# A graph layer on one core: 63 columns a chunk by the engines instead of 119, and no single rows by SP

## The chip, the cores and the metric

The kernel runs on one core of one Trainium2 chip. The core has a matrix engine (PE, TensorE), a vector engine (DVE), an activation engine (ACT), a general engine (POOL, GpSimd) and a queue engine (SP) that issues transfers and computes nothing. Each engine works through its own instructions in order; engines wait for one another through semaphores. The engines' sequencers can hold numbers in registers, and an instruction or a transfer can take its address from a register.

The metric is the time of one execution in microseconds (us), on the device. Lower is better. All times below come from the runs and the profiled execution of this kernel.

## The reference

There are 12,500 nodes with 48 features, 400,000 edges sorted by their destination, and 32 features per edge. In short:

```python
h = maximum(layernorm(x), 0)                       # 12500 x 48
tmp = concatenate([h[dst], h[src], edge_attr], 1)  # 400000 x 128
hid = relu(tmp @ W1 + b1)                          # 400000 x 128
msg = hid @ W2 + b2                                # 400000 x 48
out = x + segment_sum(msg, dst, 12500)             # 12500 x 48
```

`dst` is sorted, so that the edges of one stretch go to few nodes; `src` is random, so that each edge needs a row of its own.

## The kernel before

The product with `W1` is split by its three inputs. Two tables are made once, at the start: `tab_a` holds, for every node, `h @ W1[:48] + b1`, and `tab_b` holds `h @ W1[48:96]`. Both lie in DRAM (HBM), a row of 128 numbers (512 bytes) per node. The same numbers as `tab_b` are also kept in SBUF, turned, as `bt`: a column of 128 numbers per node.

The edges are then worked through in 391 chunks of 8 tiles, a tile being 128 edges (3125 tiles in all; the last chunk has 5). The main loop (L487 to L527) has one round per chunk `c` and two more, and it is written out in full; the order of each engine's instructions is the order in which the Python code calls them. One round touches three chunks:

- `prepare(c)` (L355) issues the loads of chunk `c`. SP loads one number (which node the chunk's window begins at), then issues the transfers for `rhs` (80 rows of `tab_a` from that node on), for the edge features into `lhs` and for the destinations (`row`). POOL issues one gather per tile: an indirect transfer of 128 rows of `tab_b`, by the tile's `src`, into `gb` (L376). DVE then makes two one-hot matrices, `lhs` (L383) and `hot` (L388).
- `before(c-1)` (L395) lets PE multiply `lhs` with `rhs` into `pre` (16 matmuls at L401): the parts of the sum that come from `dst` and from the edge features.
- `hidden(c-1)` (L415) adds the gathered rows: DVE writes `hid = pre + gb` (L420), and ACT applies the relu (L425).
- `fold(c-2)` (L428) lets PE sum the chunk's `hid` by destination within a window of 80 nodes (L433, L438), and `add(c-2)` (L443) lets DVE add that to a longer segment in SBUF (L452). Every 12 chunks a segment is multiplied with `W2`, added to `x` and stored (L456 to L484).

`gb` has six buffers (`gp`, L713). A gather for chunk `c` writes the buffer that chunk `c-6` had, so POOL can run ahead of the other engines until it has to wait for DVE's `hid` of that earlier chunk.

Not all tiles are gathered by POOL. There are two other ways:

- **Columns.** For one tile in most chunks DVE and ACT fetch the 128 columns from `bt`, one instruction per edge: `columns` (L341) copies one column of `bt`, whose address is in a register, into a column of a tile `gt` (L353). PE then adds `gt` to `pre`, turned back by a matmul with the identity (`turned`, L407; L411), and ACT applies the relu to that tile straight from `pre` (L424). The numbers of the edges' source nodes stand in a table `last` in SBUF, a row per chunk, and `load` (L329) brings them into registers with one instruction per up to 32 numbers (`numbers`, L300; the instruction has line L304). `PARTS` (L55) shares 119 columns a chunk: DVE does three parts of 23, 20 and 16, ACT two of 28 and 32. The loop places each part by hand: part 0 between `lhs` and `hot`, parts 1 and 2 ahead of `hidden`, part 3 (ACT) just ahead of `hidden`, part 4 (ACT) behind it. The register loads stand a part or more ahead of the copies.
- **Rows.** For 45 further tiles SP fetches the 128 rows from `tab_b` one at a time: `rows` (L314) issues 15 transfers of 512 bytes a chunk (L322) into a tile `gs`, each address from a register, and DVE adds `gs` in `hidden` by an instruction of its own (L422).

## Time and profile before

| | |
|---|---|
| median of 3 runs | 5028.71 us (5015.86 to 5036.02) |
| profiled execution | 5046.97 us, its span 5045.2 us |
| busy share of the span: PE, DVE, ACT, POOL | 63%, 58%, 58%, 53% |
| mean granted TensorE clock | 0.643 |
| gathers by POOL (L376) | 2719 |
| one-column copies (L353): DVE, ACT | 22,928 and 23,280 |
| single rows by SP (L322) | 5760 |

In the rows of the profile a line number stands for the line of the kernel; `out<-in` names what an instruction writes and reads; `128x896 f32` is partitions by elements. A group has its count (`x2719`), then the busy time in us and the mean of one in ns, and behind the second bar the time that its engine stood idle just before its instructions, with what ended it. "issue" is written where the profile shows nothing that the engine waited for. In the order of time each row has a start and a length in us (several like instructions in a row are merged, with their count), and in brackets the idle time before it. A q behind an engine's name (DVEq) marks what the engine's sequencer does itself, such as loading registers. In a row for a stretch of time (`A:B length, ...`) five pairs follow, the busy us and the count of instructions of PE, of PE's weight loads, of DVE, of ACT and of POOL, and then the granted clock, the share of the transfer engines and GB/s. Stretches, starts and lengths are counted from the start of the span.

### The profile page before, as it was taken

The numbers are of one execution on the slowest core, as the hardware profiler recorded it, in microseconds if no ns is written. First come the engines' busy times: TensorE is split into PE (matmuls) and PEld (weight loads), VectorE is DVE, ScalarE is ACT, GpSimd is POOL, SyncE is SP. The second block draws the span as 40 slices with busy tenths as digits, with TensorE's granted clock in tenths as the row PEclk, the third lists the DMA queues.
The fourth block names the chain that finished last, engine by engine and source line by source line (L and its number), as shares of the span: only waits on it lengthen the run. The fifth ranks groups of instructions, "written<-read, shape, count | busy, mean of one in ns | idle before, by whom it ended". The sixth has DMA issues, their size and how long they took to land. (4 is left out here: it accounts for less than half of the span.)

```text
span 5045.2 us, 105760 instructions
## 1 busy us (share of the span) xinstructions
PE 3196.2 (63%) x16917; PEld 2891.6 (57%) x16917; DVE 2915.2 (58%) x24786; ACT 2927.7 (58%) x24107; POOL 2664.5 (53%) x2746
## 2 busy tenths in 40 slices
PE   6565666665666665566666665666666666666676
PEld 4555555555555555556565555556555565555565
DVE  4555555555555555565555555555555565555555
ACT  3455655655555555566565555556565566555555
POOL 5455555555555555555555555555555555555553
PEclk8666666666666666666666666666666666665656
DMA  3422222222222222222222222222222222222221
GB/s 135 123 67 69 68 66 68 68 67 68 64 65 66 68 70 67 64 68 71 67 69 69 68 67 67 69 67 69 67 67 68 69 71 68 68 66 69 66 69 51
DMA packets 202255, 354.44 MB, mean 70 GB/s; under 512 B 70322, under 2 KB 108228, under 8 KB 200276
## 3 DMA queue, kind: packets, MB, share of 16 engines
q0 software_dynamic: 87040, 178.39, 14.2%
q1 hardware_dynamic: 114256, 169.09, 11.3%
q14 instruction: 560, 4.59, 0.3%
q8 instruction: 139, 2.28, 0.2%
q10 hardware_dynamic: 260, 0.10, 0.0%
HBM read 327.84 MB, written 22.07 MB: 69 GB/s over the span
## 5 line engine op out<-in xcount | busy, mean ns | idle before, releaser
L376 POOL DMA_INDIRECT gb<-tab_b,srci x2719 | 2643.0, 972 | 2315.4 <-DVE hid L420 1319.5
L353 ACT COPY gt<-bt 128x1 f32 x23280 | 2477.9, 189 | 1893.8 <-issue 1867.1
L353 DVE COPY gt<-bt 128x1 f32 x22928 | 1704.1, 143 | 1795.4 <-issue 1750.0
L433 PE MATMUL p_g<-hot,hid 128*128 128x80 f32 x6250 | 1392.9, 414 | 1664.1 <-ACT hid L425 1585.3
L433 PEld LDWEIGHTS p_g<-hot,hid 128*128 128x128 f32 x6250 | 1313.3, 320 | 1745.7 <-ACT hid L425 1689.4
L401 PEld LDWEIGHTS pre<-rhs,lhs 112*128 112x128 f32 x6250 | 1149.6, 283 | 92.8 <-issue 85.4
L401 PE MATMUL pre<-rhs,lhs 112*128 112x128 f32 x6250 | 1171.3, 366 | 17.1 <-DVE lhs L383 17.1
L420 DVE TENSOR_TENSOR hid<-pre,gb 128x896 f32<-128x896 f32 (+2 forms) x391 | 420.8, 1076 | 6.8 <-issue 4.4
L425 ACT ACTIVATE hid<-hid 128x896 f32<-128x896 f32 (+1 forms) x391 | 370.8, 948 | 39.3 <-DVE hid L420 38.0
L411 PE MATMUL pre<-ident,gt 128*128 128x128 f32 x722 | 278.7, 489 | 112.0 <-remote 104.9
L388 DVE TENSOR_TENSOR hot<-wnum,rel 128x640 f32<-128x640 f32 x391 | 315.9, 808 | 5.1 <-issue 4.9
L383 DVE TENSOR_SCALAR lhs<-row,bw 80x1024 f32<-80x1024 int16 x391 | 306.8, 785 | 12.8 <-DMA row<-in_dst 7.9
L438 PEld LDWEIGHTS <-ones 128*128 128x128 bf16 x3125 | 291.9, 154 | 0.0
L438 PE MATMUL p_g<-hot,ones 128*128 128x80 bf16 x3125 | 283.7, 265 | 0.0
L411 PEld LDWEIGHTS pre<-ident,gt 128*128 128x128 f32 x722 | 193.4, 328 | 118.4 <-remote 110.6
L452 DVE TENSOR_TENSOR seg<-seg,p_g 128x160 f32 x391 | 125.7, 321 | 191.8 <-DVE hid L420 156.8
L424 ACT ACTIVATE hid<-pre 128x128 f32<-128x128 f32 x361 | 97.5, 270 | 86.8 <-DVE hid L420 78.4
L478 PE MATMUL p_f<-seg,w2s 128*48 128x512 f32 (+1 forms) x134 | 121.0, 1005 | 0.4 <-DVE seg L452 0.4
L479 PE MATMUL p_f<-seg,b2s 1*48 1x512 f32 (+1 forms) x134 | 95.5, 801 | 0.0
L479 PEld LDWEIGHTS p_f<-seg,b2s 1*48 1x48 f32 x134 | 13.1, 143 | 100.8 <-issue 100.8
L468 DVE MEMSET seg<- 128x944 f32 x64 | 54.1, 845 | 9.5 <-issue 0.3
L480 DVE TENSOR_TENSOR xseg<-xseg,p_f 48x512 f32<-48x512 f32 (+1 forms) x67 | 44.8, 668 | 23.3 <-PE p_f L479 22.4
(67 smaller groups left out, 306.3 us busy)
## 6 DMA issues: line engine op xcount, KB each, us to landing
gs<-tab_b SPq DMA_DIRECT2D x5760, 0.5 KB
row<-in_dst SPq DMA_DIRECT2D x390, 160.0 KB
lhs<-in_edge_t SPq DMA_DIRECT2D x390, 128.0 KB
gb<-tab_b,srci POOLq DMA_INDIRECT x2719
rhs<-tab_a SPq DMA_DIRECT2D x391, 40.0 KB
xseg<-in_x_t SPq DMA_DIRECT2D x33, 192.0 KB
out_x<-xseg SPq DMA_DIRECT2D x33, 192.0 KB
tab_b<-tab SPq DMA_DIRECT2D x3, 1280.0 KB
```

The costliest lines, as they stand in the source:

```text
L353: copy(gts[of][:, e : e + 1], bt8[:, bass.ds(at, 4)].bitcast(F32))
L376: nc.gpsimd.indirect_dma_start(out=gb[:, t, :], out_offset=None, in_=tab_b[:, :], in_offset=bass.IndirectOffsetOnAxis(ap=srci[:, c * T + t ...
L383: nc.vector.tensor_scalar(lhs[:W, : n * P], row[:, : n * P], bw[:, c : c + 1], None, op0=ALU.is_equal,)
L388: nc.vector.tensor_tensor(hot[:, :n, :], wnum.unsqueeze(1).to_broadcast([P, n, W]), rel[:, c * T : c * T + n].unsqueeze(2).to_broadcast([P ...
L401: nc.tensor.matmul(pre[:, t, :], s["lhs"][:K, t * P : (t + 1) * P], s["rhs"][:K, :], start=True, stop=c not in BYCOLS or t < n - 1,)
L411: nc.tensor.matmul(s["pre"][:, s["n"] - 1, :], gts.pop(c), ident, start=False, stop=True)
L420: nc.vector.tensor_add(h[:, :g, :], pre[:, :g, :], s["gb"][:, :g, :])
L425: nc.scalar.activation(h[:, :m, :], h[:, :m, :], AF.Relu)
L433: nc.tensor.matmul(p_g[:, 0, :], s["h"][:, t, :], s["hot"][:, t, :], start=t == 0, stop=t == n - 1)
L438: nc.tensor.matmul(p_g[:, 1, :], ones, high[:, t, 1::2], start=t == 0, stop=t == n - 1)
L452: nc.vector.tensor_add(to, to, s["p_g"])
L478: nc.tensor.matmul(p_f[:, :n], w2s, seg[:, 0, s], start=True, stop=False)
```

## The change

The single rows by SP are gone, with `ROWS0`, `RPART`, `BYROWS`, `rows`, `gs` and the sum at L422; POOL gathers those tiles. The columns become 63 a chunk instead of 119: two parts for DVE (15 and 16) and two for ACT (16 and 16). Each part fits one load of 16 registers (part 0 has the window's base as its sixteenth number). The number table becomes 69 wide instead of 140. `gt` tiles have five buffers instead of three.

The code for the columns becomes more general: a chunk may have no, one or two tiles by columns (`TURNED`, `turned_at`), and the loop runs over as many parts as there are. The loads move: part 0 is loaded just ahead of its copies instead of at the end of the round before. The loop's general lines load and copy the last DVE part (`DVE_PARTS - 1`, here part 1) behind `hidden` and at the end of the round; `load(c, 1)` in `prepare`, behind `hot`, and `columns(c, 1)` behind `prepare` stand as they were.

```diff
 PARTS = (
-    (True, 0, 23, 1), (True, 23, 20, 24), (True, 43, 16, 44),
-    (False, 59, 28, 60), (False, 87, 32, 88),
+    (True, 0, 15, 1),
+    (True, 15, 16, 16),
+    (False, 31, 16, 32),
+    (False, 47, 16, 48),
 )
...
-BASE = 120
-RPART = 15
+BASE = 64
+DVE_PARTS = sum(dve for dve, *_ in PARTS)
+BEHIND = len(PARTS) - 1
...
-WIDTH = 140
+WIDTH = 69
...
-BYROWS = tiles_of(ROWS0, RPART)
+TURNED = {c: [j for j, of in enumerate(BYCOLS) if of == c] for c in set(BYCOLS)}
+
+def turned_at(c):
+    return ((), (T - 1,), (T // 2 - 1, T - 1))[len(TURNED.get(c, ()))]
+
+def gathered_at(c):
+    return [t for t in range(min(T, NT - c * T)) if t not in turned_at(c)]
...
-        gtp = es.enter_context(tc.tile_pool(name="gtp", bufs=3))
+        gtp = es.enter_context(tc.tile_pool(name="gtp", bufs=5))
...
-            m = max(0, min(RPART, len(BYROWS) * P - (c - ROWS0) * RPART)) if c >= ROWS0 else 0
-            base, *nodes = numbers(c, BASE, 1 + m, mybir.EngineType.SP)
+            base, = numbers(c, BASE, 1, mybir.EngineType.SP)
...
-            for t in range(n - (c in BYCOLS) - (c in BYROWS)):
+            for t in gathered_at(c):
                 nc.gpsimd.indirect_dma_start(
...
+            load(c, 0)
             columns(c, 0)
...
             for c in range(NCH + 2):
                 if c < NCH:
                     prepare(c)
-                    rows(c, st[c].pop("rows"))
                 if c >= NCH:
+                    load(c, 0)
                     columns(c, 0)
+                    load(c, 1)
                 columns(c, 1)
-                load(c, 2)
-                columns(c, 2)
+                for part in range(2, DVE_PARTS - 1):
+                    load(c, part)
+                    columns(c, part)
...
-                columns(c, 3)
+                columns(c, DVE_PARTS)
+                for part in range(DVE_PARTS + 1, BEHIND):
+                    load(c, part)
+                    columns(c, part)
                 if 0 <= c - 1 < NCH:
                     hidden(c - 1)
-                load(c + 1, 0)
-                load(c, 4)
-                columns(c, 4)
+                load(c, DVE_PARTS - 1)
+                for part in range(BEHIND, len(PARTS)):
+                    load(c, part)
+                    columns(c, part)
+                load(c + 1, DVE_PARTS)
                 if 0 <= c - 2 < NCH:
                     add(c - 2)
                     if k == GQ - 1:
                         segment_next(g)
-                load(c + 1, 3)
+                columns(c, DVE_PARTS - 1)
```

In `hidden`, a chunk with no or one tile by columns has the same two or three instructions as before: one sum by DVE over the gathered tiles, one relu by ACT over them, and, where there is a tile by columns, one relu straight from `pre`.

More of the change, by code (lines that the diff above doesn't have):

```diff
@@ L50 @@
 COLS = 1
-ROWS0 = 1
 END = NT // T
 PARTS = (
-    (True, 0, 23, 1), (True, 23, 20, 24), (True, 43, 16, 44),
-    (False, 59, 28, 60), (False, 87, 32, 88),
+    (True, 0, 15, 1),
+    (True, 15, 16, 16),
+    (False, 31, 16, 32),
+    (False, 47, 16, 48),
 )
 PART = sum(n for _, _, n, _ in PARTS)
-BASE = 120
-RPART = 15
+BASE = 64
+DVE_PARTS = sum(dve for dve, *_ in PARTS)
+BEHIND = len(PARTS) - 1
 BT0 = 16512
-SEG0 = 122144
+SEG0 = 121024
 SEG_SIZE = 8 * L
-SEG, NEXT, SEG2 = 136, 137, 138
-PLACE0 = 139
-WIDTH = 140
+SEG, NEXT, SEG2 = 65, 66, 67
+PLACE0 = 68
+WIDTH = 69
 SLOTS = (NCH + 2 + P - 1) // P
@@ L263, in windows @@
             )
-        rows_at = slice(BASE, BASE + 1 + RPART)
+        rows_at = slice(BASE, BASE + 1)
         nc.vector.tensor_scalar(
@@ L267, in windows @@
         )
-        tab8, taba8 = (t.rearrange("n h -> (n h)").bitcast(U8) for t in (tab_b, tab_a))
+        taba8 = tab_a.rearrange("n h -> (n h)").bitcast(U8)
         place = PARTS[0][3] - 1
@@ L290, in windows @@
         gts = {}
-        gss = {}
         def group(c):
@@ L312, in node @@
             return n.with_bounds(min_val=0, max_val=N - 1)
-        def rows(c, nodes):
-            for k, n in enumerate(nodes):
-                e = (c - ROWS0) * RPART + k
-                of = BYROWS[e // P]
-                if of not in gss:
-                    gss[of] = gtp.tile([P, HID], F32, name="gs")
-                n = n.with_bounds(min_val=0, max_val=4 * HID * (N - 1))
-                nc.sync.dma_start(
-                    gss[of].bitcast(U8)[e % P : e % P + 1, :],
-                    tab8[bass.ds(n, 4 * HID)].rearrange("(o h) -> o h", o=1),
-                )
         regs = {}
@@ L345, in columns @@
             for k, at in enumerate(regs.pop((c, part), [])):
-                j, e = divmod((c - COLS) * PART + first + k, P)
-                of = BYCOLS[j]
+                of, e = divmod((c - COLS) * PART + first + k, P)
                 if of not in gts:
@@ L372, in prepare @@
             )
-            st[c] = dict(n=n, rows=nodes)
+            st[c] = dict(n=n)
             gb = gp.tile([P, T, HID], F32, name="gb")
-            for t in range(n - (c in BYCOLS) - (c in BYROWS)):
+            for t in gathered_at(c):
                 nc.gpsimd.indirect_dma_start(
@@ L402, in before, with added @@
                     pre[:, t, :], s["lhs"][:K, t * P : (t + 1) * P], s["rhs"][:K, :],
-                    start=True, stop=c not in BYCOLS or t < n - 1,
+                    start=True, stop=t not in turned_at(c),
                 )
-            s["pre"], s["added"] = pre, n - (c in BYCOLS)
+            s["pre"] = pre
         def turned(c):
-            if c in BYCOLS:
-                s = st[c]
-                nc.tensor.matmul(
-                    s["pre"][:, s["n"] - 1, :], gts.pop(c), ident, start=False, stop=True
-                )
+            for t, j in zip(turned_at(c), TURNED.get(c, ())):
+                nc.tensor.matmul(st[c]["pre"][:, t, :], gts.pop(j), ident, start=False, stop=True)
         def hidden(c):
             s = st[c]
-            n, m, pre = s["n"], s["added"], s["pre"]
+            n, pre = s["n"], s["pre"]
             h = wp.tile([P, T, HID], F32, name="hid")
-            g = m - (c in BYROWS)
-            nc.vector.tensor_add(h[:, :g, :], pre[:, :g, :], s["gb"][:, :g, :])
-            if g < m:
-                nc.vector.tensor_add(h[:, g, :], pre[:, g, :], gss.pop(c))
-            if m < n:
-                nc.scalar.activation(h[:, m, :], pre[:, m, :], AF.Relu)
-            nc.scalar.activation(h[:, :m, :], h[:, :m, :], AF.Relu)
+            two = len(turned_at(c)) == 2
+            half = T // 2
+            def added(x, to):
+                if not two:
+                    return x[:, :to, :]
+                return x.rearrange("p (b t) h -> p b t h", b=2)[:, :, : half - 1, :]
+            to = n - len(turned_at(c))
+            nc.vector.tensor_add(added(h, to), added(pre, to), added(s["gb"], to))
+            if two:
+                nc.scalar.activation(
+                    h[:, half - 1 :: half, :], pre[:, half - 1 :: half, :], AF.Relu
+                )
+            elif to < n:
+                nc.scalar.activation(h[:, to, :], pre[:, to, :], AF.Relu)
+            nc.scalar.activation(added(h, to), added(h, to), AF.Relu)
             s["h"] = h
@@ L823 @@
     numbers[:NCH, NEXT] = nxt
-    cols = by_tile[np.array(BYCOLS) * T + T - 1].reshape(-1)
+    cols = by_tile[[c * T + turned_at(c)[TURNED[c].index(j)] for j, c in enumerate(BYCOLS)]].reshape(-1)
     cols = np.pad(cols, (0, -len(cols) % PART)).reshape(-1, PART)
@@ L827 @@
         numbers[COLS : COLS + len(cols), at : at + n] = cols[:, k : k + n]
-    in_rows = np.array(BYROWS) * T + T - 1 - np.isin(BYROWS, BYCOLS)
-    rows = by_tile[in_rows].reshape(-1)
-    rows = np.pad(rows, (0, -len(rows) % RPART)).reshape(-1, RPART)
-    numbers[ROWS0 : ROWS0 + len(rows), BASE + 1 : BASE + 1 + RPART] = rows
     last = np.ascontiguousarray(numbers.reshape(SLOTS, P, WIDTH).transpose(1, 0, 2))
```

## The prediction

> **What bounds the kernel now.** I read the page's engine and group rows first, then POOL's groups over the main loop, then the order of time in one chunk.

> ```profile
> span 5045.2 us, 105760 instructions
> PE 3196.2 (63%) x16917; PEld 2891.6 (57%) x16917; DVE 2915.2 (58%) x24786; ACT 2927.7 (58%) x24107; POOL 2664.5 (53%) x2746
> ...
> L353 ACT COPY gt<-bt 128x1 f32 x23280 | 2477.9, 189 | 1893.8 <-issue 1867.1
> L353 DVE COPY gt<-bt 128x1 f32 x22928 | 1704.1, 143 | 1795.4 <-issue 1750.0
> ...
> gs<-tab_b SPq DMA_DIRECT2D x5760, 0.5 KB
> ```

> No engine is full. DVE and ACT lose some 1.8 ms each in front of one-column copies, and "issue" means that the profile shows nothing they waited for. The next rows are POOL's: its only group between 160 and 4983 us, and the first gathers of the first and of the last chunk that it serves there.

> ```profile
> L376 POOL DMA_INDIRECT gb<-tab_b,srci x2671 | 2597.3, 972 | 2280.8 <-DVE hid L420 1319.5 <-issue 696.5 <-DVE hid L422 165.9
> 160.00 1.02 POOL L376 DMA_INDIRECT gb<-tab_b,srci  x1 [54.35 <-DVE hid L420]
> 4982.88 0.94 POOL L376 DMA_INDIRECT gb<-tab_b,srci  x1 [3.25 <-DVE hid L422]
> ```

> From 160.00 to 4982.88 lie 384 chunks: 4822.9 / 384 = 12.56 us each. POOL's share of one is 2597.3 / 384 = 6.76 us of gathers, 696.5 / 384 = 1.81 us of pauses of 0.30 us between them, and the rest of its idle time, (2280.8 - 696.5 - 54.35) / 384 = 3.98 us, in which it waits until DVE's sum `hid` frees a gather buffer. 6.76 + 1.81 + 3.98 = 12.55: a chunk is **a burst of gathers plus a wait for DVE**. A gather with its pause is (2597.3 + 696.5) / 2671 = 1.233 us. What DVE does meanwhile stands in the order of time of one chunk (start, length, engine, line):

> ```profile
> 3004.75 0.95 POOL L376 DMA_INDIRECT gb<-tab_b,srci  x1 [5.19 <-DVE hid L420]
> 3012.32 0.95 POOL L376 DMA_INDIRECT gb<-tab_b,srci  x1 [0.30 <-issue]
> 3017.59 0.94 POOL L376 DMA_INDIRECT gb<-tab_b,srci  x1 [4.32 <-DVE hid L420]
> 3008.39 0.81 DVE L353 COPY gt<-bt 128x1 f32 x8
> 3009.72 0.15 DVE L353 COPY gt<-bt 128x1 f32 x1 [0.52 <-issue]
> 3014.76 0.34 DVE L353 COPY gt<-bt 128x1 f32 x4 [0.55 <-issue]
> 3015.26 1.06 DVE L353 COPY gt<-bt 128x1 f32 x16 [0.16 <-issue]
> 3016.24 1.08 DVE L420 TENSOR_TENSOR hid<-pre,gb 128x896 f32<-128x896 f32 x1
> 3009.71 0.19 ACT L353 COPY gt<-bt 128x1 f32 x1 [0.45 <-issue]
> 3014.76 2.52 ACT L353 COPY gt<-bt 128x1 f32 x26 [0.51 <-issue]
> ```

> Some 4.2 us after the burst's start (3004.75 to about 3009) DVE and ACT fall into a **slow spell**: single copies, on both engines at the same instants. It ends at 3014.76 on both, 1.49 us after the last gather's end (3012.32 + 0.95). Then DVE has 20 copies left (4 and 16), 1.48 us up to `hid`; `hid` takes 1.08, and POOL starts 0.27 us after it: 1.49 + 1.48 + 1.08 + 0.27 = 4.32, the wait in the third row. Is the spell made by gathers, or by SP's single rows? Three stretches (length; then per engine busy us and count; POOL's is the fifth): a spell with rows, a spell of chunk 385 or later, when the rows are all loaded, and two chunks after the last gather.

> ```profile
> 3008.98:3014.75 5.77, 1.59 (x13) 1.40 (x13) 1.26 (x10) 1.63 (x10) 3.37 (x4) 0.50 0.23 59
> 4975.03:4980.98 5.95, 1.59 (x10) 1.40 (x8) 1.16 (x14) 2.08 (x15) 3.69 (x4) 0.50 0.21 58
> 4993.95:5009.40 15.45, 11.53 (x84) 11.15 (x84) 12.94 (x126) 12.69 (x119) 0.00 (x0) 0.79 0.08 21
> 4970.91 1.22 POOL L376 DMA_INDIRECT gb<-tab_b,srci  x1 [3.83 <-DVE hid L420]
> ```

> Without gathers there is no spell, and a chunk takes 15.45 / 2 = 7.7 us. Without rows the spell stays: 14 and 15 instructions of DVE and ACT in 5.95 us instead of 10 and 10 in 5.77, and the chunk from 4970.91 to 4982.88 takes 11.97 us. So it belongs to the gathers.

> **The change, part by part.** *More gathers.* 361 tiles by columns and 45 by rows become 191 by columns: 389 chunks of 63 columns are 24,507, in tiles of 128. POOL gathers 3125 - 191 = 2934 tiles instead of 2719. Of these 2888 fall to the 385 chunks served from 160 us on (the first six chunks come before): 7.50 a chunk instead of 6.95, 9.25 us instead of 8.57. Nothing hides this, as bursts of 6, 8 and then 7 show:

> ```profile
> 4909.84 1.47 POOL L376 DMA_INDIRECT gb<-tab_b,srci  x1 [4.79 <-DVE seg L452]
> 4920.35 0.95 POOL L376 DMA_INDIRECT gb<-tab_b,srci  x1 [2.79 <-DVE hid L420]
> 4933.97 0.95 POOL L376 DMA_INDIRECT gb<-tab_b,srci  x1 [3.84 <-DVE hid L420]
> ```

> The 6 take 10.51 us from start to start, the 8 take 13.62: the spell only ends after the last gather, so DVE cannot use a longer burst.

> *Fewer copies, but not so few.* The new loop loads and copies part 1 twice: its load stays behind `hot`, the copy stands in front of `hid`, and with two DVE parts the general lines load and copy it again behind `hid`. DVE does 15 + 16 + 16 = 47 copies a chunk, not 31, with three loads of 16 numbers; ACT does 32, with two. DVE's program without a spell is this:

> ```profile
> 4992.26 1.22 DVE L420 TENSOR_TENSOR hid<-pre,gb 128x1024 f32<-128x1024 f32 x1
> ...
> 5000.29 1.08 DVE L420 TENSOR_TENSOR hid<-pre,gb 128x896 f32<-128x896 f32 x1
> 5001.89 0.32 DVE L452 TENSOR_TENSOR seg<-seg,p_g 128x160 f32 x1 [0.52 <-DVE hid L420]
> ...
> 5002.79 1.47 DVE L353 COPY gt<-bt 128x1 f32 x23
> ...
> 5005.09 1.30 DVE L353 COPY gt<-bt 128x1 f32 x20
> 5006.90 1.07 DVE L353 COPY gt<-bt 128x1 f32 x16 [0.51 <-issue]
> 5007.87 1.09 DVE L420 TENSOR_TENSOR hid<-pre,gb 128x896 f32<-128x896 f32 x1
> ```

> From `hid` to `hid` it is 7.58 us. A copy is 0.060 us (1.47 us for 23, each lasting 0.14 and overlapping the next), so 12 fewer save 0.72. The gaps of 0.52 and 0.51 are loads of registers:

> ```profile
> L304 DVEq TENSOR_LOAD <-last x1202: 305/1382/5174, 147.5 to 5032.2; - x172
> L304 ACTq TENSOR_LOAD <-last x776: 1695/1932/2829, 134.8 to 5009.0; - x194
> ```

> (Minimum, median, maximum in ns.) ACT's loads have 28 and 32 numbers, so a number costs (1932 - 1695) / 4 = 59 ns; DVE's have 24, 20 and 16, the median being that of 20. Sixteen take 1382 - 4 × 59 = 1.15 us. Behind `hid` 8 fewer numbers close the gap of 0.52 (0.47 saved); in the other places a load stays beside `lhs`, `hot` or copies, and I save nothing. The program is 7.58 - 0.72 - 0.47 = 6.39 us, of which 6.39 - 1.35 = 5.0 lies behind the burst's start (`hid` starts 1.35 before it). [...]

> So at the spell's start (4.2) DVE has 5.0 - 4.2 = 0.8 us left, about 13 copies, where the spell lets 10 (with rows) to 14 (without) through. Bounds for the 1.48 us that now follow the spell: they go whole, or stay whole if a spell starting earlier passes less. I take zero, the nearer end by this count. ACT finishes its 32 copies likewise, and PE no longer waits for late columns.

> *SP's rows* (14.7 per chunk, behind `rhs`, `lhs` and `row` of the same chunk on SP) go. Nothing waits on SP; the chunk without rows bounds the gain at 12.56 - 11.97 = 0.6 us and the loss at nothing. It has a spell and a leftover of its own, which I have already struck out, so I add nothing. With the rows goes L422, 45 sums in all. *A wider sum*: `hid` has 1024 columns in half the chunks, 1.22 us instead of 1.08: 1.15 on average. *Set-up*, the half-sized number table and two more `gt` buffers: off the loop, zero.

> **Sum.** Wait 1.49 + 0 + 1.15 + 0.27 = 2.91; chunk 9.25 + 2.91 = 12.16 instead of 12.55; 384 × 12.16 = 4669, with 160 us before and 62.3 behind the loop 4892, with 1.8 outside the span 4893. The profiled execution took 5046.97 against a median of 5028.71 (0.4% more), about what one run differs from the next: I forecast 4890.

> **Rivals.** *A: bursts join and the spell deepens (slower).* If `hid` slips out inside the spell, the next burst starts before the spell is over, and DVE's next program meets it from its first copy. Before the loop 44 gathers ran without a break:

> ```profile
> 78.11 2.04 PE L181 MATMUL p_n<-wa,ht 97*128 97x256 f32 x4 [2.22 <-DVE bt L211]
> 87.65 0.59 ACT L190 COPY tab<-p_n 128x512 f32<-128x512 f32 x1 [13.89 <-remote]
> 104.70 0.95 POOL L376 DMA_INDIRECT gb<-tab_b,srci  x1 [0.30 <-issue]
> 109.41 0.59 ACT L190 COPY tab<-p_n 128x512 f32<-128x512 f32 x1 [21.17 <-remote]
> ```

> ACT started 7.5 us after PE's matmuls that it waits for ended (78.11 + 2.04), and the last lag outlived the gathers (104.70 + 0.95) by 3.8 us. If a second burst passes almost nothing, two chunks cost 18.5 + 3.8 + 5.3 (the program without `hid`) + 1.42 = 29.0, 14.5 each, 5790 us; if it passes copies at the usual 10 per 5.77 us, about half the program is done and the pair costs some 24.2, as forecast. Between them, 13.2 a chunk: 5290. It decides once `hid` ends within 1.49 us of the burst's last gather. Against it: no such join in the loop now.

> *B: the wait stays 3.98 (slower).* DVE's and ACT's copies run denser ahead of the spell, it starts earlier, 20 copies stay behind it: 9.25 + 3.98 = 13.23, 5300 us. Break-even is a wait of 12.55 - 9.25 = 3.30.

> *C: no spell (much faster).* The program ends at 5.0; were the spell 1 us later, POOL alone would bound: 384 × 9.3 + 222 = 3790. The rowless chunk speaks against it.

> **Chances.** Forecast with its neighbours (11.4 to 12.45 a chunk, 4600 to 5005) 0.48; A 0.26, B 0.12, C 0.07, no change 0.07. Under 0.5% a measurement of this kernel tells nothing from no change. Range 4590 to 5320; faster 0.55, same 0.07, slower 0.38. The likeliest case's own range is 4600 to 5005.

> **What would show it.** Per chunk: 7.5 gathers; a wait of POOL near 2.9 us; DVE with 0 to 3 copies between spell and `hid`; 47 DVE copies; L304 on DVE near 1.15 us; no gap over 0.15 behind `hid`. I am wrong if bursts of 15 appear (A), if ten or more copies follow the spell (B), or if spells are gone (C).

## The result, and the profile after

The changed kernel takes 5329.71 us (median of four runs, 5326.27 to 5334.81) where the kernel before, beside it, takes 5032.36 (5015.86 to 5038.81): a ratio of 1.0597, with a 95% interval of 1.0569 to 1.0625. It is 6% slower; the forecast was 4890.

In the changed kernel the loop's lines are: gathers L374, copies L352, register loads L317, `lhs` L381, `hot` L387, `hid` L425, the sum into the segment (`seg`) L459. The page of the profiled execution (5331.86 us), engines first, then groups (busy us, mean ns | idle time before them and what ended it):

```profile
span 5330.1 us, 78242 instructions
PE 3224.0 (60%) x16577; PEld 2897.8 (54%) x16577; DVE 2487.8 (47%) x20052; ACT 1731.3 (32%) x13073; POOL 2961.6 (56%) x2961
...
L374 POOL DMA_INDIRECT gb<-tab_b,srci x2934 | 2940.1, 1002 | 2289.7 <-DVE hid L425 1298.0
...
L352 DVE COPY gt<-bt 128x1 f32 x18240 | 1275.0, 144 | 1721.0 <-issue 1673.6
...
L459 DVE TENSOR_TENSOR seg<-seg,p_g 128x160 f32 x391 | 125.5, 321 | 777.5 <-issue 665.7
```

A quarter of the instructions is gone, 2934 tiles are gathered and DVE makes 18,240 copies (47 a chunk), the last two as forecast. Yet POOL waits for DVE's `hid` about as long as before, DVE idles in front of its copies about as long (1721 us, 1795 before), though it has a fifth fewer, and a new idle time stands in front of `seg`, right behind `hid`: 666 us of "issue", 1.7 us a chunk.

The whole is a mean over two different parts. POOL's group in two stretches, one ahead of chunk 128 and one behind it:

```profile
L374 POOL DMA_INDIRECT gb<-tab_b,srci x873 | 873.4, 1000 | 528.2 <-issue 232.0 <-DVE hid L425 183.2 <-DVE seg L459 57.5
L374 POOL DMA_INDIRECT gb<-tab_b,srci x1680 | 1688.0, 1005 | 1416.3 <-DVE hid L425 958.3 <-issue 452.9 <-DMA gb<-tab_b,srci 5.2
```

The first is from 200 to 1600 us: 873 / 7.5 = 116.4 chunks in 1400 us, **12.03 us a chunk**, with a wait of (528.2 - 232.0) / 116.4 = 2.54. The second is from 1800 to 4900: 1680 / 7.5 = 224 chunks in 3100 us, **13.84 us a chunk**, the wait (1416.3 - 452.9) / 224 = 4.30. DVE's register loads in two short stretches show when it changes (minimum, median, maximum in ns; first and last start):

```profile
L317 DVEq TENSOR_LOAD <-last x20: 311/1147/1153, 1607.4 to 1679.1; - x20
L317 DVEq TENSOR_LOAD <-last x9: 3601/3605/3860, 1681.5 to 1717.7; - x9
```

Up to 1679.1 us a load of 16 numbers takes 1.15 us; from the next load on, at 1681.5, it takes 3.6, and so it stays to the end (the median behind 1800 us is 3710). ACT's loads change as well, from 1042 to 3560. One chunk of the slow part, DVE's instructions in order of time (start, length, engine, line, count, idle time before):

```profile
4005.70 1.21 DVE L425 TENSOR_TENSOR hid<-pre,gb 128x1024 f32<-128x1024 f32 x1
4009.38 0.32 DVE L459 TENSOR_TENSOR seg<-seg,p_g 128x160 f32 x1 [2.47 <-issue]
4009.61 1.05 DVE L352 COPY gt<-bt 128x1 f32 x16
4010.59 0.74 DVE L381 TENSOR_SCALAR lhs<-row,bw 80x1024 f32<-80x1024 int16 x1
4014.07 1.00 DVE L352 COPY gt<-bt 128x1 f32 x15 [2.75 <-issue]
4014.99 0.81 DVE L387 TENSOR_TENSOR hot<-wnum,rel 128x640 f32<-128x640 f32 x1
4018.29 1.06 DVE L352 COPY gt<-bt 128x1 f32 x16 [2.48 <-issue]
4019.26 1.08 DVE L425 TENSOR_TENSOR hid<-pre,gb 128x896 f32<-128x896 f32 x1
```

Three loads, three gaps of about 2.5 us: behind `hid`, behind `lhs`, behind `hot`. A load begins while instructions ahead of it still run (the three here at 4005.07, 4010.35 and 4014.56, taking 4.22, 3.63 and 3.64 us), so that 0.9 to 1.8 us of it are covered and the rest is not. The copies themselves run 16 in 1.05 us, with no slow spell; behind 1800 us only 2 of DVE's 10,499 copies have a break of over 0.3 us between them and the copy ahead, where up to 1600 us 526 of 5471 have one. DVE's own program is the bound: 7.7 us of gaps and 5.8 of work make a chunk of 13.5.

What happens at chunk 128? The table of numbers, `last`, is a tile of 128 partitions; chunk `c` has its row in partition `c % 128`, and the rows of chunks 128 to 255 lie behind those of 0 to 127 in the same partitions. This place in the row, `c // 128`, is called a slot here. A row has WIDTH numbers of 4 bytes. Before, WIDTH was 140, so that slots began at bytes 0, 560, 1120 and 1680, all multiples of 16. With 69 they begin at 0, 276, 552 and 828: 0, 4, 8 and 12 modulo 16. That was the first theory (L): a register load that starts off a multiple of 16 bytes is slow. The rival (R) was anything else that comes late in the run.

### The profile page after: what moved, and what is told of

The parts are those of the page before. It is cut to its first block, busy times and chain, and to the rows that moved or that the text cites. A ratio compares the mean times of both kernels' runs of the same rounds, so it can differ in the third digit from the quotient of the medians.

```text
span 5330.1 us, 78242 instructions
## 1 busy us (share of the span) xinstructions
PE 3224.0 (60%) x16577; PEld 2897.8 (54%) x16577; DVE 2487.8 (47%) x20052; ACT 1731.3 (32%) x13073; POOL 2961.6 (56%) x2961
## 3 DMA queue, kind: packets, MB, share of 16 engines
q1 hardware_dynamic: 102736, 165.97, 10.5%
## 4 chain that ended last, share of the span: by engine, by line
issue 45%; DVE 29%; PE 13%; DVEq 5%; another core or an unknown queue 2%; POOL 1%; ACT 1%; DMA 0%; ACTq 0%; POOLq 0%
DVE gt L352 16%; PE p_g L440 6%; DVEq L317 5%; PE pre L400 5%; DVE hot L387 4%; DVE hid L425 4%; DVE lhs L381 4%; DVE seg L459 2%; POOL gb L374 1%; PE p_g L445 1%; PE p_f L485 1%; PE p_f L486 1%; PE pre L409 0%; DVE seg L475 0%
## 5 line engine op out<-in xcount | busy, mean ns | idle before, releaser
L374 POOL DMA_INDIRECT gb<-tab_b,srci x2934 | 2940.1, 1002 | 2289.7 <-DVE hid L425 1298.0
L440 PE MATMUL p_g<-hot,hid 128*128 128x80 f32 x6250 | 1422.2, 421 | 1877.4 <-ACT hid L432 1537.7
L352 DVE COPY gt<-bt 128x1 f32 x18240 | 1275.0, 144 | 1721.0 <-issue 1673.6
L352 ACT COPY gt<-bt 128x1 f32 x12416 | 1261.0, 187 | 1477.6 <-issue 1466.4
L400 PE MATMUL pre<-rhs,lhs 112*128 112x128 f32 x6250 | 1261.6, 379 | 134.7 <-issue 118.9
L400 PEld LDWEIGHTS pre<-rhs,lhs 112*128 112x128 f32 x6250 | 1198.2, 291 | 223.3 <-issue 210.4
L425 DVE TENSOR_TENSOR hid<-pre,gb 128x896 f32<-128x896 f32 (+1 forms) x391 | 449.7, 1150 | 174.8 <-issue 130.1
L459 DVE TENSOR_TENSOR seg<-seg,p_g 128x160 f32 x391 | 125.5, 321 | 777.5 <-issue 665.7
L431 ACT ACTIVATE hid<-pre 128x128 f32<-128x128 f32 x191 | 53.0, 278 | 1041.6 <-DVE hid L425 1029.1
L387 DVE TENSOR_TENSOR hot<-wnum,rel 128x640 f32<-128x640 f32 x391 | 318.5, 814 | 11.0 <-issue 10.1
L381 DVE TENSOR_SCALAR lhs<-row,bw 80x1024 f32<-80x1024 int16 x391 | 290.9, 744 | 10.6 <-DMA row<-in_dst 8.9
L409 PE MATMUL pre<-ident,gt 128*128 128x128 f32 x382 | 146.0, 485 | 5.2 <-DVE gt L352 4.1
L409 PEld LDWEIGHTS pre<-ident,gt 128*128 128x128 f32 x382 | 101.5, 325 | 7.9 <-issue 5.3
```

The lines of the kernel that those rows point to most:

```text
L352: copy(gts[of][:, e : e + 1], bt8[:, bass.ds(at, 4)].bitcast(F32))
L374: nc.gpsimd.indirect_dma_start(out=gb[:, t, :], out_offset=None, in_=tab_b[:, :], in_offset=bass.IndirectOffsetOnAxis(ap=srci[:, c * T + t ...
L381: nc.vector.tensor_scalar(lhs[:W, : n * P], row[:, : n * P], bw[:, c : c + 1], None, op0=ALU.is_equal,)
L387: nc.vector.tensor_tensor(hot[:, :n, :], wnum.unsqueeze(1).to_broadcast([P, n, W]), rel[:, c * T : c * T + n].unsqueeze(2).to_broadcast([P ...
L400: nc.tensor.matmul(pre[:, t, :], s["lhs"][:K, t * P : (t + 1) * P], s["rhs"][:K, :], start=True, stop=t not in turned_at(c),)
L409: nc.tensor.matmul(st[c]["pre"][:, t, :], gts.pop(j), ident, start=False, stop=True)
```

## Experiments: where a register load begins

**Rows of 72 numbers.** Only the length of a table row (its pitch) is changed, to 288 bytes, and with it the address of the segments that lie behind the table:

```diff
-SEG0 = 121024
+SEG0 = 121056
-WIDTH = 69
+WIDTH = 72
```

> The changed kernel, but a row of the number table is 72 numbers wide instead of 69, so a slot of 128 chunks starts at a multiple of 288 bytes (of 16 bytes) instead of 276. Theory L (register loads are slow where a slot does not start at a multiple of 16 bytes): the loads of 16 numbers on DVE and ACT take about 1.1 and 1.05 us in all four slots, the chunk stays near 12.1 us after chunk 128 too, and the time is 160 + 384 x 12.1 + 64 = 4870 us (4800 to 4930). If 64 bytes were needed, slots 1 and 3 would stay slow: about 5100. Rival R (something else goes wrong after 128 chunks, such as the clock or the order of the work): loads of 3.6 us and 5330 us as before.

Measured: 4838.75 us against 5037.22, a ratio of 0.9598 (0.9544 to 0.9652). Padding a row by three unused numbers turns a loss of 6% into a gain of 4%. DVE's loads, ACT's loads, and POOL's group from 1800 to 4700 us:

```profile
L317 DVEq TENSOR_LOAD <-last x1201: 304/1123/3412, 153.0 to 4828.1; - x172
L317 ACTq TENSOR_LOAD <-last x776: 1004/1041/2298, 137.9 to 4807.4; - x194
...
L374 POOL DMA_INDIRECT gb<-tab_b,srci x1809 | 1807.3, 999 | 1094.7 <-issue 479.6 <-DVE hid L425 393.7 <-DVE seg L459 117.2
```

The loads take 1.1 us throughout, and late in the run too a chunk takes 2900 / (1809 / 7.5) = 12.02 us. The account closes: in the changed kernel the slow loads begin at 1681 us and the last load at 5318; these 3637 us at 13.84 are 263 chunks, each 1.82 too long, 479 us; 5330 - 479 = 4851 for the span, against 4840.6.

**Rows of 70 numbers.** Slots start at 0, 8, 0 and 8 modulo 16:

```diff
-WIDTH = 69
+WIDTH = 70
```

> The changed kernel with rows of 70 numbers: slots start at 0, 280, 560 and 840 bytes, that is at 0, 8, 0 and 8 modulo 16 and at 0, 24, 48 and 8 modulo 64. Theory L: loads of 3.6 us in slots 1 and 3 alone, chunks of 12.1, 13.8, 12.1 us in slots 0, 1, 2: 160 + 250 x 12.1 + 134 x 13.8 + 64 = 5100 us. If a start at a multiple of 8 bytes is enough: 4870 and no slow load. If 64 bytes are needed, or if the cause is the late part of the run (R): slow from slot 1 to the end, 5330.

Measured: 5087.35 us. DVE's loads in slots 0, 1 and 2 (200 to 1600, 1760 to 3410 and 3530 to 4900 us):

```profile
L317 DVEq TENSOR_LOAD <-last x359: 307/1124/1324, 199.2 to 1591.9; - x180
...
L317 DVEq TENSOR_LOAD <-last x367: 308/3710/4465, 1760.9 to 3406.6; - x184
...
L317 DVEq TENSOR_LOAD <-last x353: 304/1124/1325, 3530.5 to 4899.9; - x177
```

Fast, slow, fast again in one run (and chunks of 12.0, 13.9 and 12.0 us): it isn't lateness. A start at 8 modulo 16 is slow (3710 ns), and slot 2, at 560 bytes (48 modulo 64), is fast (1124), so 64 bytes are not needed.

**The kernel before with rows of 141 numbers.** The same fault, put into the other kernel:

```diff
-SEG0 = 122144
+SEG0 = 122176
-WIDTH = 140
+WIDTH = 141
```

> The kernel before with rows of 141 numbers instead of 140: slots start at 0, 564, 1128, 1692 bytes, that is at 0, 4, 8 and 12 modulo 16. Theory L: from slot 1 on a number costs about 225 ns instead of 65, DVE's loads of 24, 20 and 16 numbers 5.4, 4.5 and 3.6 us, ACT's of 28 and 32 6.3 and 7.2; with 1.1 us of each hidden DVE's program is about 17 us, so chunks of 12.55 in slot 0 and of 17 to 19 in slots 1 and 2: 6200 to 6800 us. Rival R: 5030 us as before, loads as before.

Measured: 6421.47 us. Loads on DVE in slot 0, and on DVE and ACT from 1760 to 4900 us:

```profile
L304 DVEq TENSOR_LOAD <-last x343: 304/1381/2380, 201.2 to 1598.7; - x172
...
L304 DVEq TENSOR_LOAD <-last x546: 306/4616/6311, 1760.0 to 4897.4; - x182
L304 ACTq TENSOR_LOAD <-last x354: 5950/6634/7385, 1765.8 to 4895.7; - x177
```

One unused number more per row costs this kernel 27%. DVE's middle load, 20 numbers, goes from 69 to 231 ns a number, and chunks from 12.6 to 17.7 us.

**Parts shifted inside an even row.** Rows of 80 numbers, but DVE's part 1 begins at number 17 and ACT's second part at number 54:

```diff
-    (True, 15, 16, 16),
-    (False, 31, 16, 32),
-    (False, 47, 16, 48),
+    (True, 15, 16, 17),
+    (False, 31, 16, 36),
+    (False, 47, 16, 54),
```

> Rows of 80 numbers, so that every slot starts at a multiple of 16 bytes, but two of the four parts inside a row do not: DVE's part 1 starts at number 17 (68 bytes, 4 modulo 16) and ACT's second part at number 54 (216 bytes, 8 modulo 16); DVE's part 0 (0) and ACT's first (36, 144 bytes) do. If it is the first byte of each load that counts: in all slots one in three of DVE's loads takes 1.1 us and two (part 1 is loaded twice) 3.6, one of ACT's 1.05 and one 3.5; from the first chunk on, with one gap of 2.5 us fewer than in the changed kernel, 11.3 to 13 us a chunk, 4560 to 5220. If it is the slot's start, or the table's pitch: all loads 1.1 us and the time of the kernel with rows of 72, 4840.

Measured: 4528.39 us. Of DVE's loads 387 took 0.7 to 1.4 us and 777 over 3.3; of ACT's 387 and 388. It is the place of each single load that counts, not the table's pitch. And it is the load's first byte, not its last: for chunk 389 DVE's part 0 has only 5 numbers left to load. With rows of 72 that load begins at a multiple of 16 and ends 4 behind one, and takes 608 ns; in the changed kernel it begins 12 behind a multiple and ends at one, and takes 1184. In the kernel before, DVE's part 1 for chunk 389 has 13 numbers left, begins at a multiple and ends 4 behind one, and takes 1115. (This run was on a chip where the kernel before takes 3569 us, of which more below; its chunks are 11.3 us long.)

## Experiments: the spell, the second copy and the number of columns

**Part 1 copied once.** The changed loop loads and copies DVE's part 1 twice. From the kernel with rows of 72, the second time is taken out:

```diff
-                load(c, DVE_PARTS - 1)
...
-                columns(c, DVE_PARTS - 1)
```

> The kernel with rows of 72 numbers, and the second load and copy of DVE's part 1 (behind hid) left out: DVE copies 31 columns a chunk with two loads instead of 47 with three. Theory N (the slow spell comes when the engines have issued a certain number of instructions since the burst began, and lets them pass slowly until the gathers end): 16 copies fewer take 1.3 to 1.6 us off the wait, chunk 10.5 to 10.8, 4260 to 4370 us. Theory S (the spell starts 4.2 us after the burst whatever was issued): DVE's program to hid is through before it, POOL gathers almost without a wait, 9.3 to 9.8 a chunk, 3800 to 3990. Rival T (the spell's end alone sets hid, whatever stands in front of it): no gain, 4870 like the wider table alone.

Measured: 4982.94 us, 0.9896 of the kernel before (0.984 to 0.9952), on the chip where the kernel with rows of 72 took 4838.75. All three expectations fail: sixteen copies and a load of pure waste go, and the kernel gets 3% slower. Sorting POOL's gathers into bursts (a pause over 0.7 us ends one) shows how. With part 1 copied twice, of 357 bursts behind the first 25 are joined ones of 15; copied once, 162 of 218 are. TensorE in such a joined burst, in order of time:

```profile
2502.21 2.10 PE L440 MATMUL p_g<-hot,hid 128*128 128x80 f32 x14
2505.39 0.23 PE L440 MATMUL p_g<-hot,hid 128*128 128x80 f32 x1 [1.09 <-issue]
2506.14 0.47 PE L440 MATMUL p_g<-hot,hid 128*128 128x80 f32 x1 [0.51 <-issue]
2508.24 0.23 PE L445 MATMUL p_g<-hot,ones 128*128 128x80 bf16 x1 [1.63 <-issue]
2510.36 0.23 PE L445 MATMUL p_g<-hot,ones 128*128 128x80 bf16 x1 [1.90 <-issue]
2511.76 0.22 PE L445 MATMUL p_g<-hot,ones 128*128 128x80 bf16 x1 [1.17 <-issue]
```

The spell takes TensorE too: fourteen matmuls in 2.10 us, then one in 0.8 to 2.1 us. The prediction told of it on DVE and ACT alone. DVE's shorter program lets `hid` out earlier, POOL starts the next eight gathers without a break, and the second half of the 15 finds all three engines in the spell: in this burst ACT's copies come singly or in pairs from 2503 us on, DVE's from 2510 on, and `hid` starts at 2516.32, when TensorE's L409 is through. From burst to burst a joined pair takes 24.72 us here; in the kernel with rows of 72 a burst of 7 takes 10.64 to the next and one of 8 13.19, 23.83 together, and a joined pair 25.49.

**Fewer instructions on TensorE.** In that kernel, of the eight products with ones only the first is made:

```diff
-            for t in range(n):
+            for t in range(1):
                 nc.tensor.matmul(
-                    p_g[:, 1, :], ones, high[:, t, 1::2], start=t == 0, stop=t == n - 1
+                    p_g[:, 1, :], ones, high[:, t, 1::2], start=True, stop=True
```

> The kernel with part 1 copied once, and of TensorE's eight small products with ones per chunk (the sums of hot) only the first: seven matmuls and seven weight loads a chunk fewer, so the second half of its sums, that for the bias, is incomplete. Theory P (in the joined bursts of the kernel with part 1 copied once DVE waits for TensorE, whose instructions come singly in the spell): chunk 10.5 to 11.6 instead of 12.45, 4260 to 4680 us. Rival (TensorE does not set the pace): 4980 us as that kernel.

Measured: 4695.84 us where the kernel before took 4971.28 (0.945, against 0.990 for the kernel with all eight on its chip); 11.66 us a chunk, where the kernel with all eight took 12.39. The gain, 0.7 us by the chunks and 0.6 by the two ratios, is under the 0.85 to 1.95 that was expected: TensorE's instructions set part of the pace in joined bursts, not all of it. What sets the rest was not tested.

**No columns at all.** Every tile is gathered, and the copies and their loads are gone (the four entries of `PARTS` have 0 numbers):

```diff
-    (True, 0, 15, 1),
-    (True, 15, 16, 16),
-    (False, 31, 16, 32),
-    (False, 47, 16, 48),
+    (True, 0, 0, 1),
+    (True, 0, 0, 16),
+    (False, 0, 0, 32),
+    (False, 0, 0, 48),
```

> The kernel with rows of 72 numbers and no columns at all: every tile is gathered, 8.1 a chunk, no copies on DVE and ACT, one load of one number a chunk on DVE. If the spell needs the copies (engines with few instructions have none): POOL alone bounds, 384 x 8.13 x 1.25 + 222 = 4120 us or a little more. If gathers slow TensorE's instructions too once they run without a break: chunks of 11 to 13 us, 4450 to 5200 us, with bursts of 16 and more and TensorE's matmuls coming singly.

Measured: 4989.92 us where the kernel before takes 4971.28. TensorE again, and POOL's first gather behind a burst of 24:

```profile
2514.51 0.29 PE L440 MATMUL p_g<-hot,hid 128*128 128x80 f32 x1 [1.81 <-issue]
2515.91 0.29 PE L440 MATMUL p_g<-hot,hid 128*128 128x80 f32 x1 [1.11 <-issue]
2518.70 0.29 PE L440 MATMUL p_g<-hot,hid 128*128 128x80 f32 x1 [2.51 <-issue]
...
2524.67 1.44 POOL L374 DMA_INDIRECT gb<-tab_b,srci  x1 [7.00 <-DVE seg L459]
```

Without any copies the spell is there, on TensorE: bursts of 24 gathers, 37.5 us for three chunks, 7 us of them POOL's wait. So the spell needs no copies. It seems to hold up whichever engine still has many instructions to issue, but that is a reading of these traces and not a test.

**95 and 111 columns.** DVE keeps its 47 copies, now of 47 different columns; ACT makes 48, or 64 (`PARTS` of 95 columns; for 111 one more line of ACT's):

```diff
     (True, 15, 16, 16),
-    (False, 31, 16, 32),
+    (True, 31, 16, 32),
     (False, 47, 16, 48),
+    (False, 63, 16, 64),
+    (False, 79, 16, 80),
-WIDTH = 69
+WIDTH = 104
```

> Rows of 104 numbers (slots at multiples of 416 bytes, of 16), and 95 columns a chunk: DVE still makes 47 copies with three loads, but of 47 different columns, ACT 48 with three loads instead of 32. POOL gathers 7.26 tiles a chunk instead of 7.50. If the wait stays at the 2.8 us of the kernel with rows of 72: chunk 7.26 x 1.233 + 2.8 = 11.75, 160 + 384 x 11.75 + 64 = 4740 us. Rival: ACT's 16 further copies come through the spell slowly and the wait goes back towards 3.98: up to 12.9 a chunk, 5190 us.

> As the kernel with 95 columns, with a fourth load of 16 numbers on ACT: 111 columns, rows of 120 numbers (480 bytes), ACT 64 copies, 7.13 gathers a chunk. Wait kept at 2.8: 8.79 + 2.8 = 11.6 a chunk, 4680 us. Rival (ACT, with as many copies as in the kernel before, sets the wait): 8.79 + 3.98 = 12.77, 5130 us.

Measured: 95 columns 4770.52 us, 0.9595 of the kernel before on that chip (0.9565 to 0.9625); 111 columns 4884.78, 0.9826 (0.9795 to 0.9857). With 95 the wait stays (2.7 us, chunks of 11.85); with 64 copies on ACT the wait is 3.0 and a chunk 12.1, between the 11.6 of a kept wait and the rival's 12.77, and the saved gathers are lost again.

## Experiments: a chip without spells

Here 63, 79 and 95 columns stand side by side, all with rows of a multiple of 16 bytes, on the chip of the shifted kernel above. The 79 columns are 47 on DVE and 32 on ACT:

```diff
     (True, 15, 16, 16),
-    (False, 31, 16, 32),
+    (True, 31, 16, 32),
     (False, 47, 16, 48),
+    (False, 63, 16, 64),
-WIDTH = 69
+WIDTH = 88
```

> Rows of 88 numbers (352 bytes), 79 columns: DVE 47 different columns instead of 31 and 16 again, ACT 32. Instructions as in the kernel with rows of 72, but 7.38 gathers a chunk instead of 7.50. If the second copy of part 1 was only lost work: 0.12 x 1.27 us a chunk less, 384 x 0.16 = 60 us, 4780 us. Rival (the order of the copies matters more than the gathers): 4840 or more.

> The kernel with rows of 72 numbers again, to stand beside the others on one chip: 0.96 of the kernel before.

> The kernel with 95 columns again, beside the kernel with rows of 72 on one chip. From the two profiles (chunks of 11.87 and 12.04 us) 1.4% less than that one; the two ratios so far, 0.9595 and 0.9598, say no difference.

Measured: the kernel before takes **3569.07 us** on this chip (seven runs, 3562 to 3576), not 5030. The three take 3762.39 with 79 columns (1.0545, 1.0525 to 1.0566), 3828.61 with rows of 72 and 63 columns (1.0732, 1.0711 to 1.0753) and 3700.78 with 95 (1.0372, 1.0351 to 1.0392). All are slower than before, in proportion to their gathers: 3829 / 7.50, 3762 / 7.38 and 3701 / 7.26 are each 510 us per gather a chunk, and 3569 / 6.95 is 514. What 79 columns do where there are spells was not measured.

Two more occasions followed, with the kernels unchanged.

> The changed kernel itself, on another occasion. On a chip with slow spells (the kernel before near 5000 us): ratio 1.06 as found. On a chip without them (the kernel before near 3570 us): the three loads of 3.6 us still stand one behind the other on DVE, 13.8 a chunk from chunk 128 on, POOL's 9.4 before that: 140 + 122 x 9.4 + 262 x 13.8 + 64 = 4970 us, ratio 1.39.

> The kernel with rows of 72 numbers. With slow spells 0.96 of the kernel before, about 0.905 of the changed kernel; without them 1.07 of the kernel before (7.50 gathers a chunk against 6.95), as on the last chip.

> The kernel with 95 columns. With slow spells between 0.945 and 0.96 of the kernel before, and not slower than the kernel with rows of 72 beside it; without them 1.037.

> The kernel before, for a trace of its own on this chip. With slow spells 12.55 us a chunk with single copies in front of hid; without them about 8.9 a chunk, POOL's 6.95 gathers of 1.24 us in an unbroken row and DVE waiting for gathered rows.

Measured, on a chip with spells: the kernel before 5053.94 us, the changed kernel 5334.42 (1.055, 1.0513 to 1.0588), rows of 72 4841.21 (0.9569, 0.9534 to 0.9604), 95 columns 4777.55 (0.9451, 0.9416 to 0.9486). The last two are now side by side: 95 columns are 1.3% faster than 63, and their runs (4776 to 4786, 4836 to 4847) don't overlap. The kernel before, traced there, has 12.5 us a chunk.

> The changed kernel once more. If this chip has no slow spells (the kernel before near 3570 us): 9.4 us a chunk to chunk 128, 13.8 from there on, 4970 us. If it has them: 5330.

> The kernel before, for a trace beside it. Without spells 3570 us, 8.9 a chunk, POOL's gathers in an unbroken row; with them 5030 and 12.55.

Measured, on a fifth chip, again one without spells: the kernel before 3568.52 us, the changed kernel 4931.91, a ratio of 1.3824 (1.3784 to 1.3864). POOL's group there in the kernel before, from 200 to 3450 us, and in the changed kernel, from 200 to 1250 and from 1400 to 4780:

```profile
L376 POOL DMA_INDIRECT gb<-tab_b,srci x2537 | 2477.8, 977 | 773.7 <-issue 746.2 <-DMA gb<-tab_b,srci 18.9 <-DVE gt L353 4.6
```

```profile
L374 POOL DMA_INDIRECT gb<-tab_b,srci x823 | 801.4, 974 | 250.8 <-issue 238.0 <-DMA gb<-tab_b,srci 6.7 <-DVE gt L352 5.2
...
L374 POOL DMA_INDIRECT gb<-tab_b,srci x1840 | 1844.8, 1003 | 1536.0 <-DVE hid L425 1034.4 <-issue 492.6 <-DMA gb<-tab_b,srci 9.0
```

Without spells POOL hardly ever waits for DVE in the kernel before: of 773.7 us of idle time 746.2 are the 0.3 us between gathers, and a chunk is 3250 / (2537 / 6.95) = 8.90 us. DVE there, in the kernel before, goes from `hid` to `hid` with all its copies in dense rows:

```profile
2502.54 1.09 DVE L420 TENSOR_TENSOR hid<-pre,gb 128x896 f32<-128x896 f32 x1
2504.29 0.32 DVE L452 TENSOR_TENSOR seg<-seg,p_g 128x160 f32 x1 [0.66 <-DVE hid L420]
2504.53 0.74 DVE L383 TENSOR_SCALAR lhs<-row,bw 80x1024 f32<-80x1024 int16 x1
2505.19 1.47 DVE L353 COPY gt<-bt 128x1 f32 x23
2506.59 0.80 DVE L388 TENSOR_TENSOR hot<-wnum,rel 128x640 f32<-128x640 f32 x1
2507.50 1.39 DVE L353 COPY gt<-bt 128x1 f32 x20
2509.67 1.06 DVE L353 COPY gt<-bt 128x1 f32 x16 [0.79 <-issue]
2511.20 1.09 DVE L420 TENSOR_TENSOR hid<-pre,gb 128x896 f32<-128x896 f32 x1 [0.47 <-DMA gb<-tab_b,srci]
```

The changed kernel has 1050 / (823 / 7.5) = 9.57 us a chunk while its loads start evenly, and 3380 / (1840 / 7.5) = 13.78 behind, the same as where there are spells (13.84): DVE, held by its loads, is then the bound whatever the gathers do.

## Why the prediction was wrong

**The step that failed** is the smallest of the sum: "the half-sized number table ... off the loop, zero". The table's width is not off the loop, since it sets at which byte each load of the loop begins. The price beside it, "Sixteen take 1382 - 4 × 59 = 1.15 us", was read from a kernel whose rows are a multiple of 16 bytes and whose loads of a part all begin at one, but for a single load. In the changed kernel it measured 1.12 us in slot 0 and 3.71 behind it. That single load stood in the prediction's own row, `305/1382/5174`, of which only the median was used: the maximum is DVE's first load, the 23 numbers of part 0 for chunk 1, which has no window base ahead of them and so begins at number 1, byte 4. At 5174 / 23 = 225 ns a number it had the slow price already (being the first may add to it: ACT's first load, from a multiple of 16, took 2829 ns where its like take 1.7 us). And "in the other places a load stays beside `lhs`, `hot` or copies" holds for the 1.1 us that such a neighbour lasts; of 3.6 us and more it leaves 2.5 to 2.75 bare, three times a chunk.

**Two prices, where the sum had one.** The prediction priced every load of the change from the median of one trace, 1382 ns for 20 numbers. In this case two prices occur: loads from a multiple of 16 bytes take 1124 / 16 = 70 ns a number, the others 3710 / 16 = 232 and, in the kernel before with rows of 141, 4616 / 20 = 231. At the second price a chunk took 13.84 us, as some 263 of the chunks did. The median of the trace was right about the kernel it came from, and the change left the conditions of that trace.

**What held, where loads were even.** Of the chunks ahead of 128, and of all in the kernel with rows of 72, the forecast was 12.16 us; they took 12.03 and 12.02. That is partly luck, as two errors cancel. A gather with its pause was 1.266 us ((873.4 + 232.0) / 873) rather than 1.233, 0.25 us a chunk more; the wait was 2.54 rather than 2.91. Its parts hold in a chunk of the first slot:

```profile
1025.51 0.56 DVE L352 COPY gt<-bt 128x1 f32 x6
1026.50 0.28 DVE L352 COPY gt<-bt 128x1 f32 x3 [0.42 <-issue]
1027.27 0.15 DVE L352 COPY gt<-bt 128x1 f32 x1 [0.49 <-issue]
1027.97 0.27 DVE L352 COPY gt<-bt 128x1 f32 x3 [0.55 <-issue]
1029.41 0.21 DVE L352 COPY gt<-bt 128x1 f32 x2 [1.17 <-DMA gb<-tab_b,srci]
1030.84 0.15 DVE L352 COPY gt<-bt 128x1 f32 x1 [1.21 <-issue]
1034.07 1.09 DVE L425 TENSOR_TENSOR hid<-pre,gb 128x896 f32<-128x896 f32 x1 [3.08 <-issue]
```

```profile
1031.24 0.94 POOL L374 DMA_INDIRECT gb<-tab_b,srci  x1 [0.30 <-issue]
1035.43 0.95 POOL L374 DMA_INDIRECT gb<-tab_b,srci  x1 [3.25 <-DVE hid L425]
```

The last 16 copies pass through the spell in small groups, none is left behind it ("I take zero" was right), and `hid` comes 1.9 us after the last gather's end. But this is a burst of 8. In the kernel with rows of 72 a burst of 8 waits 3.19 us and one of 7 1.73, an alternation that the single wait of 2.91 had not in it.

**The rivals.** A (bursts join): ten bursts of 15 in the first 128 chunks, and a pair is only 1.7 us longer than two single bursts (25.49 against 23.83, in the kernel with rows of 72), so a small loss and not the 13.2 us a chunk; the mechanism is real, as the kernel that copies part 1 once shows. B (wait 3.98, 5300 us) comes within 30 us of the result, with a wait of 4.30, but for another reason: in the slow part there is no spell and no copy behind one. C (no spell): the spells did go, from chunk 128 on, perhaps because DVE and ACT, held by their loads, issued too little to meet one (inferred, not tested); that freed nothing, as DVE was the bound by then. On two of five chips there were no spells to begin with, and the gathers that the change adds cost their full price there where the loads are even (9.57 us a chunk against 8.9): the sum's sign, even of the mended change, depends on a condition that one trace could not show to be variable.

## What to carry to other kernels

When a change alters the shape of a table from which the loop loads registers, work out the first byte of every load in every part of the run, and measure the loads at each such place; a width that looked like set-up set the inner loop's price here (1.12 us a load in slot 0, 3.71 behind it). Look at a profile in stretches that follow the program's own indices (here chunk 128) before explaining its means. And a wait that no instruction explains (here the spells, there on three of five chips) may be a condition and not a constant: a change that pays only through it should be weighed without it as well, and less waste on one engine is no gain where it only lets another engine's burst grow (4982.94 us with part 1 copied once, 4838.75 with it copied twice).
